# A deformable convolution beside a selective scan: 34 instead of 28 parts of the scan, another PSUM bank for the scan's preparation, weights moved to SBUF, a state matmul issued earlier

## The chip, the core and the metric

The kernel runs on one core of a Trainium2 chip. The metric is the device time of one execution in microseconds; the time before is the median of three runs. All tensors are float32.

## The reference, cut to what matters

Four images of 128 channels and 128 x 128 pixels go through four residual layers, each `x = x + layer(group_norm(x))`:

```python
# layer 0: deformable 3x3 convolution
out = conv3x3(x, offset_w) + offset_b            # 27 values per pixel
dy, dx = clip(out[offsets], -32, 32);  mask = sigmoid(out[mask])
sampled[c, k, h, w] = mask * bilinear(x[c], y = h - 1 + k // 3 + dy, x = w - 1 + k % 3 + dx)
y = einsum('bckhw,ock->bohw', sampled, weight)
# layer 1: 5x7 dilated convolution to 16 channels, then two channel maps
# layer 2: layer norm, depthwise convolutions, a selective scan in four directions:
for t in pixels_in_the_order_of_the_direction:
    h = h * exp(delta[t] * A) + (delta[t] * u[t]) * B[t]     # 128 channels x 16 states
    y[t] = (h * C[t]).sum(over 16 states)
#          layer norm, gate, output projection, layer norm
# layer 3: 3x3 convolution with an edge correction
```

## The kernel before

**The scan is the backbone.** `scan` walks over 4 images x 4 directions x 32 blocks = 512 blocks of 512 pixels. The 128 x 16 states of a block lie in four tiles `h` (128 partitions x 4 x 512, index j), and each tile is scanned in four pieces (index g), one DVE scan instruction each (L1079). So a block has 16 scans, called slots here. For each j the scan needs:

- the input product `h = du * B`: `states_up` (L929) makes the matrix B's rows in the PSUM tile `dub` by two matmuls, and `inputs` (L936) multiplies it into `h`. Three of four run on DVE; the fourth runs on GpSimd (POOL) with a B loaded into SBUF (`bb`), or on DVE as well, see below.
- the decay `exp(delta * A)`: one ACT instruction per slot into a PSUM tile `pa` (L966). Two `pa` banks rotate; a third bank (bank 3) joins them when the work beside the scan leaves it free.
- after its four scans: `carry_on` (L997), the product with C in `outputs` (L1003, `h * cb`, both tiles in SBUF), and `sums` (L977, matmuls into `yacc`).

`prepare(t + 2)` computes delta and delta * u of a later block in small steps, one at each `next(more)`, with three PSUM uses in turn (L873, L889, L901), a copy by ACT (L905) and a product on POOL (L908).

**Beside the scan run the other layers.** They are Python generators, and `together` pulls them in proportion: `around(b)` lists, for each image's 128 blocks, the stages beside them with a weight ("parts"). Beside image 0's scan stand the rest of its own layer2_pre (18 parts), image 1's table (12), and layer 0, layer 1 and layer2_pre of image 1 (28, 14, 36); beside images 1 and 2 stand `tail` of the image before (layer2_post 16, layer 3 with the next table 34) and `head` of the next. A stage gets blocks in the ratio of its parts to the sum. The program order of every engine is then fixed by the order in which the instructions were recorded; nothing is rescheduled at run time, engines wait for each other by semaphores.

`loads("POOL", layer0(st))` sets `beside["busy"] = "POOL"` while layer 0 runs, and the scan then takes DVE instead of POOL for the fourth input product, for `carry_on` and for `outputs` (`c["by"] = nc.vector`). `loads(..., True)` sets `beside["spare"]`, which says that bank 3 may be used by the scan.

**Layer 0** goes over 288 taps (32 blocks of four rows x 9 kernel positions, index n), in a weave of steps:

- `gather`: two tiles `g` of 128 x 2 x 4 x 128, each filled by two indirect DMAs that POOL issues (L447), and for the tap two before, one corner's weighting on POOL (L455);
- `weigh_upper` on ACT (L468), `weigh_lower` on DVE: two instructions per tap, `g[lower] * wl` (L479), where `wl` holds the lower corners' weights of a strip of 16 rows. `lower_weights` (L428) writes `wl` into PSUM bank 2;
- `turn` on TensorE: 16 transposing matmuls (L490) into bank 1 or 3, `copy` by ACT into `smp` (L502), `project` (L510) into bank 0, `add` on DVE (L517, L518) after nine taps.

Ten `g` tiles rotate (20 in the prologue), so POOL can run ahead of the others by some taps. `positions(j + 1)` computes the next strip's sampling points in small steps on TensorE (L359, bank 3), ACT and DVE.

**PSUM.** Eight banks: `dub`, two `pa`, `yacc`, and banks 0 to 3 for the work beside. While layer 0 runs (`beside["full"]`) it holds all four, and `prepare` shares `dub` with `states_up`:

```python
own = beside["own"] = bool(beside.get("spare")) and not beside.get("full")
def place(name):
    return bank(3, name) if own else pss.tile([P, N], F32, name=name, tag="dub")
```

So with `own` false the state matmul for j + 1 is issued at g == 3, one slot ahead, and `sums` at g == 1; with `own` true they are issued at g == 2 and g == 3.

**The prologue** computes layer 0 of image 0 without a scan beside it (L447 to L518 as above), then its layer 1 and the start of layer2_pre; the first scan instruction starts at 2298.6 us.

Of the kernel before, what the change touches and what calls it, by code (L numbers as in the profile page):

```python
# [10 lines left out]
F32 = mybir.dt.float32  # L11
# [7 lines left out]
P = 128  # L19
# [4 lines left out]
N = R * W  # L24
NBLK = H // R
KK = 9
# [5 lines left out]
NG = 4  # L32
# [8 lines left out]
ROWS = 16  # L41
# [71 lines left out]
def conv_preact_kernel(ctx: ExitStack, tc: tile.TileContext, a: dict, nb: int):  # L113
    nc = tc.nc
# [13 lines left out]
    def bank(which, name):  # L128
        return psb.tile([P, N], F32, name=name, tag=f"bank{which}")
# [182 lines left out]
    def layer0(st, pairs=10):  # L312
# [5 lines left out]
        with ExitStack() as s:  # L318
# [18 lines left out]
            def positions(j):  # L337
# [4 lines left out]
                y0 = j * ROWS  # L342
                xs, base, top = got["s", j]

                got["third"] = True
                po = bank(3, "po")
                po3 = po.rearrange("p (r w) -> p r w", w=W)
# [76 lines left out]
            def lower_weights(j):  # L424

                wts = got.pop(("l", j))
                wl = bank(2, "wl")[:, 0 : 2 * ROWS * KK]
                nc.vector.tensor_mul(  # L428
                    wl.rearrange("p (q n) -> p q n", q=2),
                    wts[:, 1:2, 0].to_broadcast([P, 2, ROWS * KK]), wts[:, :, 1],  # L430
                )
                got["p"] = wl.rearrange("p (q r b k) -> p r b k q", q=2, r=R, b=BPS)
# [105 lines left out]
                yield None  # L538
            flush()
            beside["full"] = True  # L540
            while beside.get("own") or beside.get("third"):
                yield None
            fetch_strip(0)
            for n, _ in enumerate(positions(0)):
# [6 lines left out]
                yield share + (1.0 - share) * f  # L551
            flush()
            beside["full"] = False
        st["x1"], st["stats1"] = keep, stats_out


# [260 lines left out]
    def scan(pull):  # L817
# [35 lines left out]
        def prepare(t, early=False):  # L853

            st, k, i, back = seq[t]
            c = blocks[t]
            if (st["b"], k) not in carries:
                carries[st["b"], k] = carry = small.tile([P, NST], F32, name="carry")
                nc.vector.memset(carry, 0.0)
            c["carry"] = carries[st["b"], k]  # L860
            c["bc"] = st["bc"][k % 2][i, k // 2]
            u = c["u"]
            own = beside.get("own")
            beside["prepares"] = own

            def place(name):
                return bank(3, name) if own else pss.tile([P, N], F32, name=name, tag="dub")

            yield None
            if own:  # L870
                yield None
            pdt = place("pdt")
            nc.tensor.matmul(pdt, wd[:, k, :], u, start=True, stop=True)  # L873
            yield None

            dtb = col(V_DTB + k)
            e = sp.tile([P, N], F32, name="e", bufs=1)
            nc.scalar.activation(e, pdt, AF.Abs, bias=dtb)
            above = sp.tile([P, N], F32, name="above", bufs=1)
            nc.scalar.activation(above, pdt, AF.Relu, bias=dtb)  # L880
            yield None
            nc.scalar.activation(e, e, AF.Exp, scale=-1.0)
            yield None
            one_e = sp.tile([P, N], F32, name="one_e", bufs=1)
            nc.scalar.activation(one_e, e, AF.Identity, bias=1.0)
            yield None
            if not back:
                px = place("pxbc")
                nc.tensor.matmul(px, xbc[:, k, :], u, start=True, stop=True)  # L889
            ln = sp.tile([P, N], F32, name="ln", bufs=1)  # L890
            nc.scalar.activation(ln, one_e, AF.Ln)
            yield None
            if not back:
                bc = sp.tile([4 * NST, N], F32, name="bc", bufs=1)
                nc.scalar.copy(bc, px[0 : 4 * NST])  # L895
                store(st["bc"][k][i].rearrange("d j s t -> (d j s) t"), bc)
            nc.scalar.activation(one_e, one_e, AF.Identity, bias=minus)  # L897
            yield from slots(1 if own else 2 if early else 4)
            pd = place("psum")
            for n, (t, sign) in enumerate(((e, ident), (one_e, less), (ln, ident), (above, ident))):  # L900
                nc.tensor.matmul(pd, sign, t, start=n == 0, stop=n == 3)  # L901
            yield from slots(1 if early else 2)
            steps = sp.tile([P, 2, N], F32, name="steps", bufs=1)
            delta, du = steps[:, 0, :], steps[:, 1, :]
            nc.scalar.copy(delta, pd)  # L905
            beside["prepares"] = False
            yield from slots(2 if early else 1)
            nc.gpsimd.tensor_mul(du, delta, u)  # L908
            c["steps"] = sd = dram.tile([P, 2 * N], F32, name="stepsd", bufs=4)
            store(sd, steps.rearrange("p j t -> p (j t)"), 2)  # L910
# [41 lines left out]
        def decay(n):  # L952

            t, n = divmod(n, NST)
            j, g = divmod(n, NG)
            k = seq[t][1]
            turn = (ahead["turn"] + 1) % 3
            if turn == 2 and (not beside.get("own") or beside.get("prepares")):
                turn = 0
            ahead["turn"] = turn  # L960
            if turn == 2:
                beside["third"] = beside.get("third", 0) + 1
                blocks[t]["third", n] = True
            pa = bank(3, "pa3") if turn == 2 else pss.tile([P, N], F32, name="pa", bufs=2)
            at = g * NG + j
            nc.scalar.activation(pa, blocks[t]["d", g], AF.Exp, scale=neg_a[:, k, at : at + 1])  # L966
            blocks[t]["a", n] = pa
# [54 lines left out]
        for t, (st, k, i, back) in enumerate(seq):  # L1022
            c = blocks[t]
            carry = c["carry"]
            on_vector = beside.get("busy") == "POOL"
            own = beside["own"] = bool(beside.get("spare")) and not beside.get("full")
            c["by"] = nc.vector if on_vector else nc.gpsimd
            more = prepare(t + 2, on_vector) if t + 2 < len(seq) else iter(())
            if t > 0:
# [1 line left out]
            for j in range(NG):  # L1031
# [16 lines left out]
                for g in range(NG):  # L1048
                    n = j * NG + g
                    if g == 1:  # L1050
                        decays(at + 1)
                        if t + 1 < len(seq) and j == 3:
                            spread_steps(t + 1, 2)
                            spread_steps(t + 1, 3)
                        if t + 1 < len(seq) and j == (2 if c["by"] is nc.gpsimd else 3):
                            spread_products(t + 1)
                        next(more, None)
                        if before[0] >= 0:
                            carry_on(*before, c["by"])
                            outputs(*before, c["by"])  # L1060
                        if earlier[0] >= 0 and not own:
                            sums(*earlier)
                        if own and j == 2 and t > 0:
                            finish(t - 1)
                    if n and g in (0, 3):
                        next(more, None)
                    if g == 3 and not own and then[0] < len(seq) and not (then[1] == NG - 1 and c["by"] is nc.gpsimd):
                        states_up(*then)
                    if g == 2:
                        decays(at + 2)  # L1070
                        if j == 0 and c["by"] is nc.gpsimd:
                            inputs(t, NG - 1, nc.gpsimd)
                        next(more, None)
                        if own and then[0] < len(seq) and not (then[1] == NG - 1 and c["by"] is nc.gpsimd):
                            states_up(*then)
                    o, f = h[:, g, :], c["a", n]
                    if back:
                        o, f = o[:, ::-1], f[:, ::-1]
                    nc.vector.tensor_tensor_scan(o, f, o, carry[:, n : n + 1], ALU.mult, ALU.add)  # L1079
                    if ("third", n) in c:  # L1080
                        beside["third"] -= 1
                    if g == 3:
                        decays(at + 3)
                        if own and earlier[0] >= 0:
                            sums(*earlier)
                        if not own and j == 1 and t > 0:
                            finish(t - 1)
                    yield (t * NST + n + 1) / total
# [295 lines left out]
    def loads(engine, stage, spare=False):  # L1384
        for f in stage:
            beside["busy"], beside["spare"] = engine, spare
            yield f
        beside["busy"], beside["spare"] = None, False

    def head(b):  # L1390
        st = sts[b]
        table = [(loads(None, layer0_table(st), True), 12)] if b < 2 else []
        return table + [(loads("POOL", layer0(st)), 28), (loads("PE", layer1(st), True), 14),
                (loads("PE", layer2_pre(st), True), 36)]

    def tail(b):
# [117 lines left out]
```

## Time and profile before

| | us |
|---|---|
| median of three runs (20785.77 to 20800.34) | 20786.91 |
| the profiled execution | 20838.75 |
| its span, first to last instruction | 20837.0 |
| mean granted TensorE clock | 0.892 |

| stretch of the span, us | what runs beside the scan | blocks |
|---|---|---|
| 0 to 2298.6 | prologue, no scan | - |
| 2298.6 to 3413.1 | rest of layer2_pre (image 0), table (image 1) | 36 |
| 3413.1 to 5348.7 | layer 0 of image 1 | 33 |
| 5348.7 to 7074.1 | layer 1 and layer2_pre of image 1 | 59 |
| 7074.1 to 8596.4 | layer2_post and layer 3 of image 0, table of image 2 | 51 |
| 8596.4 to 10514.1 | layer 0 of image 2 | 28 |
| 10514.1 to 11986.0 | layer 1 and layer2_pre of image 2 | 49 |
| 11986.0 to 13508.2 | layer2_post and layer 3 of image 1, table of image 3 | 51 |
| 13508.2 to 15424.6 | layer 0 of image 3 | 28 |
| 15424.6 to 16894.4 | layer 1 and layer2_pre of image 3 | 49 |
| 16894.4 to 20837.0 | the last image's scan, layer2_post, layer 3 | 128 |

How to read what follows: PE is TensorE, PEld its weight loads, DVE is VectorE, ACT ScalarE, POOL GpSimd. L447 is line 447 of the kernel before. A row of a stage shows its busy time on each engine with the number of instructions, then the granted clock, the DMA engines' share and GB/s. A group's row shows busy time, the mean of one instruction in ns, and the idle time before the group with what ended it. A timeline row shows start, duration, the instruction and, in brackets, the idle time before it.

### The profile page before, as it was taken

Reading aid. Unit: us, or ns where it says so; the run is one execution under the profiler, and the core shown is the slowest. Engines: PE = TensorE matmul, PEld = TensorE weight load, DVE = VectorE, ACT = ScalarE, POOL = GpSimd, SP = SyncE. Lnnn points to the kernel's source line nnn. Section 1 sums busy time; section 2 is a strip of 40 time slices with the busy share of each in tenths; the row PEclk is TensorE's granted clock in tenths of the full one; section 3 lists DMA queues with packets and bytes.
Section 4 is the critical chain, followed back from the end, with each engine's and each line's share of the span. In section 5 each row is a group of like instructions: output and inputs, shape, how many; then the busy total and the mean of one; then the engine's idle time right before and its main releaser. Section 6 shows DMA issues by size and latency. Waiting matters only on the chain.

```text
span 20837.0 us, 209864 instructions
## 1 busy us (share of the span) xinstructions
PE 15847.0 (76%) x58778; PEld 6719.5 (32%) x58778; DVE 16855.7 (81%) x14665; ACT 12887.2 (62%) x25086; POOL 16827.5 (81%) x10597
## 2 busy tenths in 40 slices
PE   4667776777878888777778887877777877677778
PEld 2444222444322223344422222244432222122223
DVE  1222588888999899888899889978889998999983
ACT  3444566666667666566667776666666767655563
POOL 4775577888788888888878888888878889999994
PEclk7888888998989999899999998988998988899899
DMA  7666678777767877777777796777776777555673
GB/s 234 192 193 191 193 229 283 259 255 253 245 205 225 235 236 254 239 247 251 247 235 224 225 250 229 253 244 248 248 241 221 235 216 221 185 185 195 197 219 120
DMA packets 2909354, 4717.50 MB, mean 226 GB/s; under 512 B 1095248, under 2 KB 1369240, under 8 KB 2831264
## 3 DMA queue, kind: packets, MB, share of 16 engines
q1 hardware_dynamic: 2539552, 3495.83, 52.5%
q0 software_dynamic: 368640, 1208.25, 18.8%
q8 instruction: 476, 7.80, 0.1%
q14 instruction: 686, 5.62, 0.1%
HBM read 3766.27 MB, written 908.60 MB: 224 GB/s over the span
## 4 chain that ended last, share of the span: by engine, by line
DVE 34%; PE 19%; issue 12%; DMA 11%; ACT 10%; POOL 8%; another core or an unknown queue 3%; SPq 2%; DVEq 0%; POOLq 0%; ACTq 0%
DVE h L1079 20%; DVE h L936 11%; PE pst L490 4%; PE psum L901 4%; POOL g L447 3%; DMA du<-stepsd 3%; ACT pa L966 3%; DMA g<-table,idx 2%; PE acc L510 2%; ACT g L468 2%; DMA delta<-stepsd 2%; PE p L1309 1%; POOL h L1003 1%; PE yacc L977 1%
## 5 line engine op out<-in xcount | busy, mean ns | idle before, releaser
L1079 DVE TENSOR_TENSOR_SCAN h<-pa,carry,h 128x512 f32<-128x512 f32 x8192 | 10005.1, 1267 | 767.6 <-ACT pa L966 571.5
L966 ACT ACTIVATE pa<-delta,neg_a 128x512 f32<-128x512 f32 x8192 | 5538.0, 687 | 4751.5 <-DVE h L1079 3700.4
L1003 POOL TENSOR_TENSOR h<-h,cb 128x2048 f32<-128x2048 f32 x1692 | 7670.5, 4533 | 137.0 <-POOL carry L997 0.6
L447 POOL DMA_INDIRECT g<-table,idx x4608 | 4874.2, 1058 | 1679.5 <-issue 1136.4
L936 DVE TENSOR_TENSOR h<-du,dub 128x2048 f32<-128x2048 f32 x1625 | 3684.3, 2267 | 826.4 <-PE dub L929 310.3
L490 PE MATMUL pst<-ident,g 128*128 128x128 f32 x18432 | 2670.0, 299 | 1665.1 <-issue 644.8
L929 PE MATMUL dub<-u,xb_sb 128*128 128x512 f32 x3250 | 2047.3, 716 | 1713.3 <-DVE h L936 1529.8
L490 PEld LDWEIGHTS pst<-ident,g 128*128 128x128 f32 x18432 | 2312.0, 155 | 2699.8 <-issue 1297.6
L468 ACT ACTIVATE g<-g,wt 128x128 f32<-128x128 f32 x8072 | 2577.6, 392 | 216.7 <-DMA g<-table,idx 162.4
L977 PE MATMUL yacc<-h,gather_sb 128*32 128x512 f32 x16384 | 2364.6, 650 | 87.0 <-POOL h L1003 61.0
L936 POOL TENSOR_TENSOR h<-du,bb 128x2048 f32<-128x2048 f32 x423 | 1927.4, 4557 | 18.1 <-DMA du<-stepsd 18.1
L479 DVE TENSOR_TENSOR g<-g,wl 128x512 f32<-128x512 f32 x2304 | 1488.2, 669 | 359.9 <-DMA g<-table,idx 315.4
L502 ACT COPY smp<-pst 128x512 f32<-128x512 f32 x1152 | 664.8, 577 | 1569.9 <-remote 1013.2
L929 PEld LDWEIGHTS dub<-u,xb_sb 128*128 128x128 f32 x3250 | 598.4, 210 | 2877.1 <-DVE h L936 2211.9
L510 PE MATMUL acc<-smp,w_sb 128*128 128x512 f32 x2304 | 1371.3, 679 | 133.2 <-DVE x L517 60.9
L908 POOL TENSOR_TENSOR steps<-steps,u 128x512 f32<-128x512 f32 x512 | 652.5, 1274 | 909.5 <-ACT steps L905 905.2
L1309 PE MATMUL p<-xn,w_l_sb 128*128 128x508 f32 (+2 forms) x2304 | 1149.6, 620 | 1.8 <-ACT xn L1288 1.8
L977 PEld LDWEIGHTS yacc<-h,gather_sb 128*32 128x32 f32 x16384 | 338.3, 112 | 1838.1 <-issue 1315.9
L901 PE MATMUL psum<-e,ident 128*128 128x512 f32 x1024 | 613.8, 684 | 357.6 <-ACT bc L895 338.0
L901 PE MATMUL psum<-one_e,less 128*128 128x512 f32 x1024 | 639.1, 711 | 310.7 <-ACT one_e L897 310.1
L517 DVE TENSOR_TENSOR x<-acc,xres 128x512 f32<-128x512 f32 x128 | 87.1, 680 | 966.5 <-remote 525.3
L455 POOL TENSOR_SCALAR g<-g,wt 128x128 f32<-128x128 f32 x1144 | 833.0, 728 | 37.4
(170 smaller groups left out, 18122.0 us busy)
## 6 DMA issues: line engine op xcount, KB each, us to landing
cb<-bcd SPq DMA_DIRECT2D x512, 1024.0 KB
delta<-stepsd SPq DMA_DIRECT2D x2048, 256.0 KB
du<-stepsd SPq DMA_DIRECT2D x2048, 256.0 KB
stepsd<-steps SPq DMA_DIRECT2D x512, 512.0 KB
table<-gt SPq DMA_DIRECT2D x512, 256.0 KB
bb<-bcd SPq DMA_DIRECT2D x512, 256.0 KB
win<-nd SPq DMA_DIRECT2D x512, 160.0 KB
g<-table,idx POOLq DMA_INDIRECT x4608
```

What stands on the lines that cost most here:

```text
L447: nc.gpsimd.indirect_dma_start(out=g[:, r].rearrange("p q c -> p (q c)"), out_offset=None, in_=table, in_offset=bass.IndirectOffsetOnAxis( ...
L468: nc.scalar.activation(g, g, AF.Copy, scale=w)
L479: nc.vector.tensor_mul(g, g, wl.unsqueeze(3).to_broadcast([P, 2, 2, P]))
L490: nc.tensor.matmul(pst[:, r * P : (r + 1) * P], g[:, r % 2, q, :], ident, start=q == 0, stop=q == 3, is_transpose=True,)
L510: nc.tensor.matmul(got["a", i], w0[:, k, :], got.pop(("c", n)), start=k == 0, stop=k == KK - 1)
L901: nc.tensor.matmul(pd, sign, t, start=n == 0, stop=n == 3)
L929: nc.tensor.matmul(p, xb[:, seq[t][1], j, :], c["u"], start=True, stop=True)
L936: engine.tensor_mul(h, c["du"], b.unsqueeze(1).to_broadcast([P, NG, N]))
L966: nc.scalar.activation(pa, blocks[t]["d", g], AF.Exp, scale=neg_a[:, k, at : at + 1])
L977: nc.tensor.matmul(c["y"][g * Q : (g + 1) * Q, :], gather, c["h", j][:, g, :], start=j == 0, stop=last and not second,)
L1003: engine.tensor_mul(h, h, c["cb"][:, j, :].unsqueeze(1).to_broadcast([P, NG, N]))
L1079: nc.vector.tensor_tensor_scan(o, f, o, carry[:, n : n + 1], ALU.mult, ALU.add)
```

## The change

Layer 0 gets 34 parts of the scan instead of 28, the other stages keep theirs. `wl` becomes an SBUF tile. Bank 2, which this frees while layer 0 runs, takes the three PSUM uses of `prepare`; `own` is now the number of the bank (2 beside layer 0, 3 where bank 3 is spare, 0 otherwise). With `own == 2` the state matmul for j + 1 is issued at g == 1, three slots before its use. `sums` and `finish` follow the branch that `own` selects, so beside layer 0 they are issued at g == 3 and at j == 2. `positions` first copies out whatever transposed tap is still in PSUM, and layer 0 ends only when a running `prepare` has left bank 2.

```diff
@@ positions
+                for n in [key[1] for key in got if key[0] == "t" and isinstance(key, tuple)]:
+                    copy(True)(n)
                 got["third"] = True
                 po = bank(3, "po")
@@ lower_weights
-                wl = bank(2, "wl")[:, 0 : 2 * ROWS * KK]
+                wl = mp.tile([P, 2 * ROWS * KK], F32, name="wl")
@@ layer0
-            while beside.get("own") or beside.get("third"):
+            while beside.get("own") == 3 or beside.get("third"):
                 yield None
...
             beside["full"] = False
+            while beside.get("own") == 2 and beside.get("prepares"):
+                yield None
@@ prepare
-                return bank(3, name) if own else pss.tile([P, N], F32, name=name, tag="dub")
+                return bank(own, name) if own else pss.tile([P, N], F32, name=name, tag="dub")
@@ decay
-            if turn == 2 and (not beside.get("own") or beside.get("prepares")):
+            if turn == 2 and (beside.get("own") != 3 or beside.get("prepares")):
@@ scan
-            own = beside["own"] = bool(beside.get("spare")) and not beside.get("full")
+            own = beside["own"] = 2 if beside.get("full") else 3 if beside.get("spare") else 0
+            beside["prepares"] = own if t + 2 < len(seq) else 0
...
                         next(more, None)
+                        if own == 2 and then[0] < len(seq):
+                            states_up(*then)
                         if before[0] >= 0:
                             carry_on(*before, c["by"])
                             outputs(*before, c["by"])
...
-                        if own and then[0] < len(seq) and not (then[1] == NG - 1 and c["by"] is nc.gpsimd):
+                        if own == 3 and then[0] < len(seq) and not (then[1] == NG - 1 and c["by"] is nc.gpsimd):
                             states_up(*then)
@@ head
-        return table + [(loads("POOL", layer0(st)), 28), (loads("PE", layer1(st), True), 14),
+        return table + [(loads("POOL", layer0(st)), 34), (loads("PE", layer1(st), True), 14),
```

## The prediction

> **What bounds the kernel now.** I read the totals, then busy time by stage, then the groups and waits inside the deformable layer, then a stretch of the timeline.
>
> ```profile
> PE 15847.0 (76%) x58778; PEld 6719.5 (32%) x58778; DVE 16855.7 (81%) x14665; ACT 12887.2 (62%) x25086; POOL 16827.5 (81%) x10597
> ```
> DVE and POOL tie as an average, so they must be parted by stage. Busy time by stage (columns: length, then PE, PEld, DVE, ACT, POOL):
>
> ```profile
> 3413.10:5348.70 1935.60, 1474.73 (x7505) 821.72 (x7505) 1701.94 (x1709) 1253.74 (x3141) 1547.07 (x1475) 0.90 0.76 249
> 5348.70:7074.10 1725.40, 1381.45 (x4113) 455.97 (x4113) 1616.84 (x1225) 1164.74 (x1839) 1490.19 (x623) 0.91 0.70 226
> 8596.40:10514.10 1917.70, 1414.08 (x7249) 794.58 (x7249) 1519.37 (x1573) 1181.15 (x3008) 1496.61 (x1470) 0.89 0.74 241
> 10514.10:11986.00 1471.90, 1217.50 (x3609) 410.21 (x3609) 1366.75 (x1030) 1013.38 (x1597) 1248.91 (x524) 0.92 0.73 232
> ```
> Rows 1 and 3 are layer 0 of images 1 and 2 beside the scan; rows 2 and 4 are layer 1 and layer2_pre behind it. Counting scans (16 to a block), they hold 33, 59, 28 and 49 blocks. Layer 0 takes the same time over 33 blocks (1935.6 us) as over 28 (1917.7): it doesn't go by blocks. The other stretch does: 1725.4 - 1471.9 = 253.5 us for ten blocks, 25.35 us each. There DVE's scans set the pace (94% busy).
>
> What holds layer 0? Its inner part, 3490 to 5300 us (1810 us), POOL's groups (busy, mean ns, idle before them):
>
> ```profile
> L447 POOL DMA_INDIRECT g<-table,idx x1118 | 1242.4, 1111 | 304.1 <-issue 244.9 <-DMA g<-table,idx 8.7 <-DVE h L1079 8.0
> L455 POOL TENSOR_SCALAR g<-g,wt 128x128 f32<-128x128 f32 x279 | 216.1, 775 | 9.1
> L908 POOL TENSOR_TENSOR steps<-steps,u 128x512 f32<-128x512 f32 x31 | 39.6, 1279 | 0.0
> ```
> Busy plus idle is 1811 us, all of it, and the idle is some 0.27 us before each gather: POOL never waits for anybody. **POOL is the bound of layer 0.** DVE in the same window:
>
> ```profile
> DVE h L936 <- PE dub L929: 69.8, 35, 8.9
> DVE h L936 <- issue: 57.8, 31, 8.0
> ```
> These waits (152 us with the smaller ones) are what the earlier state matmul is to remove, but on the engine that isn't the bound.
>
> The timeline shows what slows POOL:
>
> ```profile
> 4401.52 0.95 POOL L447 DMA_INDIRECT g<-table,idx  x1 [0.30 <-issue]
> 4403.29 3.06 POOL L447 DMA_INDIRECT g<-table,idx  x1 [0.17 <-issue]
> 4406.66 0.95 POOL L447 DMA_INDIRECT g<-table,idx  x1 [0.30 <-issue]
> ...
> 4403.18 2.29 DVE L1003 TENSOR_TENSOR h<-h,cb 128x2048 f32<-128x2048 f32 x1
> 4406.59 0.66 DVE L479 TENSOR_TENSOR g<-g,wl 128x512 f32<-128x512 f32 x1
> ```
> A gather that starts under DVE's L1003, whose two inputs (h, cb) both lie in SBUF, takes 3.06 instead of 0.95 us; one beside L479, whose wl lies in PSUM, keeps 0.95. That contrast decides this case, because the change moves wl to SBUF. In the prologue, without L1003, a gather takes 964 ns and an L455 626. So L1003 costs POOL here (1242.4 - 1118 x 0.964) + (216.1 - 279 x 0.626) = 206 us for 124 of them, 1.66 us each.
>
> **The change, part by part.** The sum starts from the profiled execution: 20838.75 us, of which 20837.0 is span; the median of the runs is 20786.91, 51.8 lower. I apply the difference to the median.
>
> *34 parts for layer 0.* In the built order the blocks with L1003 on DVE go from 33, 28, 28 to 38, 33, 33; five blocks per image leave the other stages. There each is worth 25.35 us by the two rows above; layer2_pre alone gives 25.5 (42 blocks in 1225.7 us, 35 in 1047.0). A block beside layer2_post (34 us, DVE busy 32) hangs less on the scans, so I take 24: 15 x 24 = -360 (-315 to -380). In layer 0 a block more costs POOL four L1003 and one L908: 4 x 1.66 + 1.28 = 8 us, so 40 per image; the trace's own pair gives 18 for five blocks (1935.6 against 1917.7), as a short layer 0 starts with a crowded block of 124 us. I take 40 + 25 + 25 = +90 (54 to 120).
>
> *Lower weights in SBUF.* L428 writes SBUF instead of PSUM: nothing. The 576 L479 per image now have two SBUF inputs. Duration: L936 (one input in PSUM) has a mean of 2283 ns, L1003 (both SBUF) at best 2291, so L479 stays at 0.66 to 0.69. The price is POOL's. In the trace a gather that starts at least 0.05 us into an L1003 ends as if it had started 0.12 us before the L1003's end. Laid over the recorded L479s, that rule catches some 260 of 576 per image, 0.27 us each: 70 us. Counting L479s that stand back to back as one gives 87 to 101. The short two-input operations of the position computation (0.45 us) lose POOL about 40 ns each, which by the square of the window beyond the first 0.17 us is 0.13 us for 0.69, or 75. I take 80: 3 x 80 = +240. Ends: 40 ns each, the short row unscaled (3 x 23), and 3 x 110.
>
> The Trainium skill (SBUF — State Buffer, "Who interferes with whom") says that a DVE instruction with two SBUF inputs contends with a GpSimd instruction that reads SBUF but not with one that only writes, and infers that descriptor generation needs only the write side. By that page only L455, one POOL operation in five, would be hit, an estimate of 15 us per image, and the total would be about 200 us faster. The 3.06 us gather speaks against the inference here, and the row decides.
>
> *Prologue.* Image 0's layer 0 has no scan beside it: no gain, but 576 L479. POOL there has waits of some 3 us per nine taps (2.13 and 1.37 us in one stretch), so the same 70 us is partly covered: +35 (0 to 70). DVE's L479s come there in bursts, 17 in 10.23 us after a wait for L517. Whether POOL gets in between two of a burst no row shows; that is rival C.
>
> *Preparation in bank 2, state matmul at g == 1, sums at g == 3.* These lift at most DVE's 152 us (image 1) or 224 us (image 2) of L936 waits, which POOL hides: 0. Without that cover the gain would be those waits. The matmul L929 waits for L936 of the same j, which stands before scan 0, so it is free at g == 1; behind it queue the transposes L490, and they wait for POOL anyway. The later sums hold one of five h tiles two scans longer: 0; exposed, at most the 3 us per L936 that the longer waits show.
>
> *Copies before positions* move eight ACT copies of 0.57 us per image: 0, as ACT is 66% busy; behind an early copy queue the decays, which now wait on DVE. *The wait at the end of layer 0* holds layer 1 back about 0.4 block; such a block takes 42 us instead of 26 (block 206 of before), so some 6 us per image, which the faster pull afterwards gives back: 0 (to 20).
>
> *Is DVE late next?* Image 1: 38 blocks x 39.7 us (16 x 1.275, 4 x 2.28, 4 x 2.33, carries 0.9) = 1509, L479 397, the rest of the layer 95: 2001, less 5% of overlap (the groups sum to 1690 in a window of 1605 busy) = 1900. POOL: 288 taps x 5.59 (4 x 1.234 + 0.65) = 1610, blocks 38 x 8 = 304, L479 80, ends 50: 2044. POOL stays the bound, DVE at 93%; +15 for the coupling (0 to 60).
>
> Sum: -360 + 90 + 240 + 35 + 15 = **+20 us**, 20859 profiled, **20807 as median**. About 0.2% (42 us) is what a measurement of this kernel can tell from no change.
>
> **The rivals.** *B, the lock hardly bites* (23 us an image, 10 in the prologue): -360 + 90 + 69 + 10 + 15 = -176, 20611. For it: the short two-input rows lose only 40 ns, and wl is broadcast in its last dimension, which no two-input row shows. Against: 3.06 us under L1003.
>
> *C, bursts shut POOL out* (slower): a DVE burst of two-input operations holds the shared port from one L479 to the next. Then every burst of 17 costs POOL its 10 us less 3 of slack, 32 bursts: +225 instead of +35, and 95 instead of 80 beside the scan: +45. Total 20 + 190 + 45 = +255, 21042; with the stall also slowing the chain behind, to +330. It decides as soon as a POOL operation waits longer than one L479. For it: the burst of 17; against: a gather needs the port only for a moment.
>
> *D, DVE becomes the bound of image 1*: if its 11% of waits stay, 1900 / 0.89 = 2135 against 2044, so +75 net: 20880. For it: 93% load; against: the waits shrank from 300 to 205 us where the load grew.
>
> **How the numbers follow.** A holds 0.50, its own range 20700 to 20910 (the bounds of the lock and of the price of a block); of it 0.15 falls below -0.2%, 0.17 within, 0.18 above. B 0.20 (0.19 faster, 0.01 same), C 0.25 and D 0.05 (slower). Faster 0.34, same 0.18, slower 0.48. The range reaches to B's centre and C's long end: 20600 to 21120.
>
> **What would show it.** Layer 0 of image 1 at some 2040 us over 38 blocks, of images 2 and 3 at 2020 over 33; POOL again without waits there; gathers under an L479 at 1.2 to 1.5 us where they began inside it; layer 1 plus layer2_pre at 24 to 25 us per block less. The prologue tells A from C: 2330 or 2520 instead of 2298.6 us to the first scan. A gather mean unchanged at 0.96 in the prologue would be B. I am wrong altogether if POOL waits in layer 0 or DVE's L936 waits prove to set its time.

## The result, and the profile after

The changed kernel takes 20819.23 us (median of 20 runs, 20804.16 to 20836.59), the kernel before 20786.58 in 20 runs beside it: a ratio of 1.0015, interval 1.0008 to 1.0022. The forecast was 20807 with a range of 20600 to 21120. Its profiled execution took 20823.53 us, span 20821.8, which is 4 above its median; the one of before lay 52 above its own.

The totals moved little:

```profile
PE 15832.9 (76%) x58808; PEld 6696.5 (32%) x58808; DVE 17147.3 (82%) x14800; ACT 12901.1 (62%) x25086; POOL 16903.7 (81%) x10462
```

By stage they moved a great deal. Busy time of the changed kernel by stage, the rows that answer to those of before (length, then PE, PEld, DVE, ACT, POOL): layer 0 of image 1, layer 1 and layer2_pre of image 1, and the same two of image 2.

```profile
3356.40:5427.30 2070.90, 1555.82 (x7765) 825.62 (x7765) 1914.74 (x1849) 1330.20 (x3262) 1679.47 (x1478) 0.90 0.76 245
5427.30:7051.00 1623.70, 1332.47 (x3963) 439.72 (x3963) 1535.45 (x1167) 1119.55 (x1769) 1418.36 (x595) 0.92 0.73 231
8502.90:10536.80 2033.90, 1491.18 (x7507) 815.43 (x7507) 1732.41 (x1710) 1261.67 (x3129) 1627.77 (x1475) 0.89 0.75 239
10536.80:11965.50 1428.70, 1192.79 (x3511) 407.06 (x3511) 1311.88 (x995) 984.38 (x1552) 1198.06 (x504) 0.92 0.75 233
```

All stages, from the first scan of each block:

| stage | before, us (blocks) | after, us (blocks) | difference |
|---|---|---|---|
| prologue | 2298.6 | 2273.6 | -25.0 |
| rest of layer2_pre, table | 1114.5 (36) | 1082.8 (34) | -31.7 |
| layer 0, image 1 | 1935.6 (33) | 2070.9 (38) | +135.3 |
| layer 1, layer2_pre | 1725.4 (59) | 1623.7 (56) | -101.7 |
| layer2_post, layer 3 | 1522.3 (51) | 1451.9 (48) | -70.4 |
| layer 0, image 2 | 1917.7 (28) | 2033.9 (33) | +116.2 |
| layer 1, layer2_pre | 1471.9 (49) | 1428.7 (47) | -43.2 |
| layer2_post, layer 3 | 1522.2 (51) | 1451.8 (48) | -70.4 |
| layer 0, image 3 | 1916.3 (28) | 2031.7 (33) | +115.4 |
| layer 1, layer2_pre | 1469.9 (49) | 1428.5 (47) | -41.4 |
| last scan and what follows | 3942.6 (128) | 3944.3 (128) | +1.7 |

The stages that the 15 blocks left gave 358.8 us, the three layers 0 took 366.9. So the change is two large effects that cancel.

POOL's groups in the inner part of layer 0 of image 1 (3420 to 5380 us, 1960 us; busy, mean ns, idle before them):

```profile
L449 POOL DMA_INDIRECT g<-table,idx x1130 | 1350.5, 1195 | 306.3 <-issue 220.9 <-DMA g<-table,idx 17.2 <-DVE h L1086 11.2
L457 POOL TENSOR_SCALAR g<-g,wt 128x128 f32<-128x128 f32 x283 | 249.4, 881 | 9.3
L912 POOL TENSOR_TENSOR steps<-steps,u 128x512 f32<-128x512 f32 x36 | 45.9, 1275 | 0.0
```
Busy and idle again make up the whole window, with 0.27 us of idle per gather, so POOL is still the bound; a gather now means 1195 ns instead of 1111, the corner product 881 instead of 775. DVE's waits in the same window:

```profile
DVE g L481 <- DMA g<-table,idx: 61.5, 42, 4.2
DVE h L940 <- PE dub L933: 22.8, 15, 3.0
```
The waits of the state product for `dub` fell from 70 to 23 us, and those of L481 for gathers rose from 23 to 62: DVE waits for POOL.

What a gather meets under a lower-weight product, in the timeline of the changed kernel (start, duration):

```profile
4038.37 1.03 POOL L449 DMA_INDIRECT g<-table,idx  x1 [0.31 <-issue]
4039.70 1.47 POOL L449 DMA_INDIRECT g<-table,idx  x1 [0.30 <-issue]
4041.47 1.47 POOL L449 DMA_INDIRECT g<-table,idx  x1 [0.31 <-issue]
...
4039.69 0.66 DVE L481 TENSOR_TENSOR g<-g,wl 128x512 f32<-128x512 f32 x1
4040.27 1.27 DVE L1086 TENSOR_TENSOR_SCAN h<-pa,carry,h 128x512 f32<-128x512 f32 x1
4041.46 0.66 DVE L481 TENSOR_TENSOR g<-g,wl 128x512 f32<-128x512 f32 x1
```
A gather that starts 0.01 us after an L481 takes 1.47 instead of 0.95 us. Here a product and a scan on DVE take 1.77 us, a delayed gather with its 0.30 us of issue also 1.77, so the next gather starts at the next L481 again.

That gathers crowd at the start of a product is not new, though. Of an image's 1152 gathers, 66, 53 and 65 begin within 0.05 us of an L479's start in the profile of before, and they lose nothing there, as here with 0.02 us between the two starts:

```profile
4475.63 0.95 POOL L447 DMA_INDIRECT g<-table,idx  x1 [0.30 <-issue]
...
4475.61 0.66 DVE L479 TENSOR_TENSOR g<-g,wl 128x512 f32<-128x512 f32 x1
```
In the changed kernel 102, 81 and 87 begin so, and each loses 0.51 us.

### The profile page after: what moved, and what is told of

The parts are those of the page before. It is cut to its first block, busy times and chain, and to the rows that moved or that the text cites. A ratio compares the mean times of both kernels' runs of the same rounds, so it can differ in the third digit from the quotient of the medians.

```text
span 20821.8 us, 209810 instructions
## 1 busy us (share of the span) xinstructions
PE 15832.9 (76%) x58808; PEld 6696.5 (32%) x58808; DVE 17147.3 (82%) x14800; ACT 12901.1 (62%) x25086; POOL 16903.7 (81%) x10462
## 4 chain that ended last, share of the span: by engine, by line
DVE 32%; PE 18%; DMA 14%; issue 12%; POOL 10%; ACT 9%; SPq 2%; another core or an unknown queue 2%; DVEq 0%; POOLq 0%; ACTq 0%
DVE h L1086 18%; DVE h L940 10%; POOL g L449 6%; DMA g<-table,idx 6%; PE psum L905 4%; ACT pa L970 3%; DMA du<-stepsd 3%; PE pst L492 2%; DMA delta<-stepsd 2%; PE acc L512 2%; PE p L1316 1%; ACT g L470 1%; POOL g L457 1%; DVE g L481 1%
## 5 line engine op out<-in xcount | busy, mean ns | idle before, releaser
L1007 POOL TENSOR_TENSOR h<-h,cb 128x2048 f32<-128x2048 f32 x1632 | 7398.9, 4534 | 131.8 <-POOL carry L1001 0.8
L449 POOL DMA_INDIRECT g<-table,idx x4608 | 5231.0, 1135 | 1602.8 <-issue 987.0
L492 PEld LDWEIGHTS pst<-ident,g 128*128 128x128 f32 x18432 | 2260.9, 153 | 3065.4 <-POOL g L457 1535.0
L481 DVE TENSOR_TENSOR g<-g,wl 128x512 f32<-128x512 f32 x2304 | 1634.8, 721 | 1106.4 <-DMA g<-table,idx 881.3
L940 POOL TENSOR_TENSOR h<-du,bb 128x2048 f32<-128x2048 f32 x408 | 1859.4, 4557 | 19.6 <-DMA du<-stepsd 16.3
L512 PE MATMUL acc<-smp,w_sb 128*128 128x512 f32 x2304 | 1417.4, 702 | 70.7 <-DVE x L519 42.0
L1007 DVE TENSOR_TENSOR h<-h,cb 128x2048 f32<-128x2048 f32 x416 | 954.9, 2296 | 14.3
L457 POOL TENSOR_SCALAR g<-g,wt 128x128 f32<-128x128 f32 x1144 | 905.3, 791 | 37.6
```

The lines of the kernel that those rows point to most:

```text
L449: nc.gpsimd.indirect_dma_start(out=g[:, r].rearrange("p q c -> p (q c)"), out_offset=None, in_=table, in_offset=bass.IndirectOffsetOnAxis( ...
L481: nc.vector.tensor_mul(g, g, wl.unsqueeze(3).to_broadcast([P, 2, 2, P]))
L492: nc.tensor.matmul(pst[:, r * P : (r + 1) * P], g[:, r % 2, q, :], ident, start=q == 0, stop=q == 3, is_transpose=True,)
L512: nc.tensor.matmul(got["a", i], w0[:, k, :], got.pop(("c", n)), start=k == 0, stop=k == KK - 1)
L940: engine.tensor_mul(h, c["du"], b.unsqueeze(1).to_broadcast([P, NG, N]))
L1007: engine.tensor_mul(h, h, c["cb"][:, j, :].unsqueeze(1).to_broadcast([P, NG, N]))
```

## The experiments

Each run was timed against the kernel before on the same chip. The chips differ: the kernel before has medians of 20691.79, 20821.12, 20698.84 and 20830.01 us on the four that were used, and the prologue, where its work is the same, takes 2184 to 2299 us to the first scan. So stages are compared, and totals only as ratios. "The lock" is, as in the prediction, the time that POOL is held up while DVE runs an instruction with two inputs in SBUF.

**1. The kernel before again.**

> The kernel before once more, for a second profile. The changed kernel's profile reaches the first scan at 2273.6 us, the first profile of before at 2298.6, though the changed kernel's gathers lose 61 us more there under L479. Theory 1, an edit of the change speeds the prologue up: the first scan again at about 2298 us. Theory 2, the prologue varies from one execution to the next: another time, down to about 2250 us (the first profile lay 52 us above the median of the runs). The stages after it should repeat within 5 us each under both.

The prologue took 2184.6 us instead of 2298.6; all stages after it but layer 0 repeat within 4 us, layer 0 (1929.8, 1907.5, 1908.8) only within 6 to 10, where I had expected 5. Theory 2: the prologue varies. What goes with it is seen beside the run of experiment 8, which has the same prologue work but for the early copies. First each run's busy time between 300 and 1800 us, with the granted clock third from the end, then TensorE's costliest group; experiment 1:

```profile
300.00:1800.00 1500.00, 953.22 (x5280) 638.79 (x5279) 452.92 (x716) 748.62 (x2155) 1200.39 (x1340) 0.90 0.70 203
```
```profile
L490 PE MATMUL pst<-ident,g 128*128 128x128 f32 x4288 | 640.8, 298 | 544.6 <-POOL g L455 538.3 <-ACT smp L502 6.2
```
and experiment 8:

```profile
300.00:1800.00 1500.00, 947.75 (x5052) 681.91 (x5048) 393.38 (x687) 668.40 (x2042) 1131.53 (x1264) 0.81 0.67 192
```
```profile
L492 PE MATMUL pst<-ident,g 128*128 128x128 f32 x4064 | 638.2, 324 | 438.6 <-ACT smp L504 259.0 <-issue 179.4
```
At a granted clock of 0.90 the transposes wait for POOL, which bounds the prologue; at 0.81 they wait for ACT's copies, in the loop of transposes, copy and projection, and POOL has slack. The clock was 0.81 in the first profile of before as well. That the clock is the cause is my reading of these profiles; no run sets it.

**2. 34 parts alone.**

```diff
-        return table + [(loads("POOL", layer0(st)), 28), (loads("PE", layer1(st), True), 14),
+        return table + [(loads("POOL", layer0(st)), 34), (loads("PE", layer1(st), True), 14),
```


> The kernel before with 34 instead of 28 parts for layer 0 and nothing else. Theory A (POOL bounds layer 0, five blocks per image leave the scan-bound stages): -360 there, +40 +25 +25 in layer 0 and +15 for the coupling, so about -255 us, some 20530; layer 0 of image 1 takes about 1975 us over 38 blocks, of images 2 and 3 about 1940 over 33. Theory D (DVE becomes the bound of image 1, since here the state matmul still comes one slot ahead): layer 0 of image 1 at 2080 to 2135 us, the total near -130, some 20655.

20524.07 us, 0.9917 (0.9903 to 0.9930): a gain of 168, between theory A's 255 and theory D's 130 and nearer to D. Against experiment 1 the other stages gave 369 us and layer 0 took +112.9, +40.2 and +40.2. For images 2 and 3 that is the 40 of four L1003 and one L908 per block. Image 1 took 2042.7 us, between the theories. Its waits there (3420 to 5350 us, 1930 us), POOL's and DVE's:

```profile
POOL steps L908 <- ACT steps L905: 109.6, 27, 27.5
```
```profile
DVE h L936 <- PE dub L929: 111.5, 73, 7.4
```
Here POOL does wait: for the scan's preparation, up to 27.5 us at a time, while DVE is busy 1792.48 of 1930 us and has `dub` in use late. I read this as DVE setting the time of image 1 at 38 blocks, with the preparation sharing `dub`, and dragging POOL along; no run parts DVE's load from its waits for `dub`.

**3. The lower weights in SBUF alone.**

```diff
-                wl = bank(2, "wl")[:, 0 : 2 * ROWS * KK]
+                wl = mp.tile([P, 2 * ROWS * KK], F32, name="wl")
```


> The kernel before with the lower weights in an SBUF tile and nothing else. Theory A (the second SBUF input of L479 holds POOL up): as in the changed kernel's profile, where operations of POOL that begin under an L479 lose 126, 110 and 111 us in the three images, so +330 to +350 beside the scan, in layer 0 alone, and between -27 and +60 in the prologue: 21090 to 21200. As it stood in the prediction: +275, 21062. Theory B (the lock hardly bites, the loss of the changed kernel lies in the bank or the order): within 30 us of before.

21012.99 us, 1.0158 (1.0144 to 1.0171): 321 us lost. Layer 0 took 100.0, 87.7 and 81.8 us more than in experiment 1, the prologue 47.1 more, and the sum of all other stages moved 18 us the other way. POOL's operations that begin under an L479 lose 115.6, 97.5 and 94.6 us there, those under L1003 some 20, 5 and 11 less than in experiment 1. Theory B is out. This one line and the blocks add up to the loss of the change: with the 40 us that five blocks cost images 2 and 3 of experiment 2, it makes 140, 128 and 122 us, where experiment 5 has 141.8, 124.8 and 133.4. In layer 0 it cost less than the 330 to 350 us that I expected from the first profile (269.5 in all); with the prologue it is 317, where the prediction's terms say 275.

**4. The early copies alone.**

```diff
+                for n in [key[1] for key in got if key[0] == "t" and isinstance(key, tuple)]:
+                    copy(True)(n)
```


> The kernel before with the early copy of a transposed tap before the positions and nothing else. Theory 1 (this copy frees TensorE in the prologue, where it waits 296 us for ACT's copies): the first scan some 25 us earlier, the total near -27, 20760; beside the scan nothing, as POOL is the bound. Theory 2 (the copies are worth nothing): within 10 us of before.

1.0002 (0.9993 to 1.0011), first scan at 2186.2 against 2184.6: nothing. Theory 2.

**5. The changed kernel again.**

> The changed kernel once more, for a profile from the same chip as those it is compared with here. Theory A: against the second profile of before, layer 0 of the three images longer by 140, 126 and 125 us, the prologue by 40 to 50 (as with the weights in SBUF alone, 2231.7 against 2184.6), the other stages shorter by some 360 in all, as in the first profile: +30 to +80. If the prologue of the changed kernel is really shorter by an edit, it stays 25 under that of before.

1.0010 (1.0001 to 1.0019). Layer 0 took 2071.6, 2032.3 and 2042.2 us: 141.8, 124.8 and 133.4 more than in experiment 1. The prologue, 2294.7, can't be set against that run's, whose clock was higher; experiment 8 on this chip has 2295.9 with the weights in PSUM, so here the SBUF weights cost the prologue nothing.

**6. The whole change at 28 parts.**

```diff
-        return table + [(loads("POOL", layer0(st)), 34), (loads("PE", layer1(st), True), 14),
+        return table + [(loads("POOL", layer0(st)), 28), (loads("PE", layer1(st), True), 14),
```


> The whole change, but with 28 parts. It differs from the run with the weights in SBUF alone (1.0158 of before) by the bank, the earlier state matmul and the order of the sums. Theory A (POOL covers DVE's waits, so these are worth nothing here): within 40 us of that run, 1.014 to 1.018. Theory E (the bank and the earlier matmul are worth some 70 to 100 us in every image, as the difference between 34 parts alone, the weights alone and the whole change suggests when simply added): 1.002 to 1.006.

1.0120 (1.0105 to 1.0136), below the band named for A and above E's. Layer 0 took 2029.2, 1987.6 and 1980.7 us, against 2029.8, 1995.2 and 1990.6 in experiment 3. So bank, earlier matmul and later sums are worth 0 to 10 us per image at 28 parts, as A says; most of the rest of the difference is the prologue (2295.0 us, against 2295.9 in experiment 8 with the weights in PSUM), where the lock cost nothing on this chip.

**7. The lower-weight product in two halves** (the whole change otherwise).

```diff
-                    nc.vector.tensor_mul(g, g, wl.unsqueeze(3).to_broadcast([P, 2, 2, P]))
+                    for r in range(2):
+                        nc.vector.tensor_mul(g[:, r], g[:, r], wl[:, r].unsqueeze(2).to_broadcast([P, 2, P]))
```


> The changed kernel with each product by the lower weights issued as two instructions of half the length (0.42 us instead of 0.69, 128 x 256 each). If the port is given up between two such instructions, POOL loses less per image, by the square of the window some 40 to 60 us instead of 110 in images 2 and 3: layer 0 there some 55 us shorter. If a run of two-input instructions keeps it, the pair is a window of 0.85 us and POOL loses 150 to 190: layer 0 there 40 to 80 us longer. Image 1 has 80 us more of DVE work and should be longer either way.

0.9950 (0.9937 to 0.9964): the changed kernel with more instructions beats the changed kernel by 0.6%. POOL's loss under the products fell to some 70 us per image (71, 67 and 66), layer 0 to 2034.1, 2000.1 and 1998.5. Mostly POOL gets in between two products that stand back to back: of 416 gathers beside the scan that began under a half which another half followed at once, 391 went on when the first one ended, 25 later. It isn't always so. In the prologue a run of 19 halves held one gather for 5.30 us:

```profile
442.72 6.45 DVE L482 TENSOR_TENSOR g<-g,wl 128x256 f32<-128x256 f32 x19
...
444.75 5.30 POOL L449 DMA_INDIRECT g<-table,idx  x1 [1.99 <-issue]
```
A second one took 3.80 us there, and two of 8.77 and 6.21 us stand in the prologue of experiment 12. The size is less than I expected (32 and 44 us instead of 55 in images 2 and 3), and image 1, which I held to be longer either way, is 37.5 shorter: POOL, not DVE, still set it.

**8. 34 and 42 parts, weights in PSUM** (with the copies of experiment 4).

```diff
-        return table + [(loads("POOL", layer0(st)), 28), (loads("PE", layer1(st), True), 14),
+        return table + [(loads("POOL", layer0(st)), 34 if b < 2 else 42), (loads("PE", layer1(st), True), 14),
```


> The kernel before with 34 parts for layer 0 of image 1 and 42 for images 2 and 3, weights left in PSUM, with the early copies (worth nothing by themselves). Theory A with what 34 parts alone showed: image 1 as there (layer 0 2043 us over 38 blocks); images 2 and 3 now also get 38 blocks and come to DVE's limit, some 2040 us of layer 0 (+93 against 34 parts) for five blocks less elsewhere (-117): 25 us each gained over 34 parts alone, so 0.989 of before. Rival: the stages that are left get too dense to give 23 us a block, and it is 0.992 or worse.

0.9864 (0.9849 to 0.9879), better than 34 parts alone. Layer 0 of images 2 and 3 took 2008.6 and 2006.7 us over 37 blocks (I had expected 2040 over 38), some 60 more than over 33, and the other stages kept giving (1365.2 and 1370.7 us for 45 blocks).

**9. The corner of L455 on ACT** (the kernel before otherwise).

```diff
-                    if h == 1 and n >= 2:
-                        g, w = neighbour(n - 2, h, 1, 1)
-                        nc.gpsimd.tensor_scalar(g, g, w, None, ALU.mult)
...
-                            if h == 1 and r == 1 and c == 1 and n + 2 < NBLK * KK:
-                                continue
```


> The kernel before (28 parts, weights in PSUM) with the one corner that POOL weights (L455) weighted by ACT like the other three of the upper row. Theory A (POOL is the bound of layer 0): 288 times 0.65 us and what L1003 adds to them leave POOL, so layer 0 of images 2 and 3 some 195 us shorter (1720), until DVE is the bound; image 1, where DVE is 88% busy, 110 to 150 shorter; total 0.973 to 0.978 with the prologue between 0 and -100. Rival (something else holds layer 0 at 1910 us whatever POOL does, the gathers' transfers or TensorE): within 60 us of before.

20088.58 us, 0.9709 (0.9696 to 0.9723): the best version found, faster than both kernels. Layer 0 took 1825.8, 1739.0 and 1734.2 us (-104, -169, -175 against experiment 1), the prologue 2016.8 (-168). That is more than I expected in the total (0.973 to 0.978), because of the prologue, and less in layer 0 (110 to 150 in image 1, 195 in images 2 and 3). POOL still bounds image 2, though some of its idle time now ends with ACT and with gathers' transfers (8280 to 9840 us, 1560 us), where its two groups' busy and idle make 1561:

```profile
L447 POOL DMA_INDIRECT g<-table,idx x1093 | 1194.8, 1093 | 331.3 <-issue 177.3 <-ACT g L463 29.1 <-DMA g<-table,idx 28.7
L903 POOL TENSOR_TENSOR steps<-steps,u 128x512 f32<-128x512 f32 x26 | 33.4, 1285 | 2.0 <-ACT steps L900 1.6
```

**10. The same with 30 and 36 parts.**

```diff
-        return table + [(loads("POOL", layer0(st)), 28), (loads("PE", layer1(st), True), 14),
+        return table + [(loads("POOL", layer0(st)), 30 if b < 2 else 36), (loads("PE", layer1(st), True), 14),
```

> As the run before it, with 30 parts for layer 0 of image 1 and 36 for images 2 and 3. Theory A: images 2 and 3 come to DVE's limit at 34 blocks, layer 0 some 100 us longer than with 28 parts for 144 us less elsewhere; image 1 a loss of 30. So 60 us better than the run before it, 0.970 to 0.975. Rival: DVE is already the bound there at 28 parts, every block more costs 40 us in layer 0 and gives 24 elsewhere: 150 us worse than the run before it.

0.9708 (0.9695 to 0.9722), the same as experiment 9: layer 0 took 93, 111 and 109 us more, the other stages gave as much. Both expectations missed; with POOL relieved the number of parts no longer matters around here.

**11. The state matmul one slot ahead again** (the changed kernel otherwise).

```diff
-                        if own == 2 and then[0] < len(seq):
-                            states_up(*then)
...
+                    if g == 3 and own == 2 and then[0] < len(seq):
+                        states_up(*then)
```


> The changed kernel with the state matmul beside layer 0 one slot ahead (g == 3) again, the bank kept. Theory A (POOL covers DVE's waits): layer 0 of images 2 and 3 within 10 us of the changed kernel (2032, 2042); image 1, where DVE is 94% busy, 20 to 60 us longer than 2071, as the waits of L936 come back. Rival (the earlier slot carries the difference between 34 parts alone and the whole change): image 1 longer by 70 us or more and the others by 30 or more.

Layer 0: 2072.1, 2040.5, 2034.7 us, against 2071.6, 2032.3, 2042.2 in experiment 5. DVE's waits in image 1 came back (3380 to 5330 us):

```profile
DVE h L940 <- PE dub L933: 129.5, 66, 5.2
```
and cost nothing, in image 1 neither, where I had expected 20 to 60. The earlier matmul is worth nothing here, where POOL is the bound. (The total, 1.0042 with 1.0028 to 1.0056, comes from a chip with a high clock: its prologue took 2231.5 us, as in experiment 3.)

**12. The whole change with the corner on ACT** (the edit of experiment 9 in the changed kernel).

```diff
-                    if h == 1 and n >= 2:
-                        g, w = neighbour(n - 2, h, 1, 1)
-                        nc.gpsimd.tensor_scalar(g, g, w, None, ALU.mult)
...
-                            if h == 1 and r == 1 and c == 1 and n + 2 < NBLK * KK:
-                                continue
```

> The whole change (34 parts, bank 2, weights in SBUF) with the corner of L455 weighted by ACT, so that POOL has room beside layer 0. Theory A (what the change lost was POOL's time, the bank is worth DVE's waits once DVE is the bound): POOL still loses 90 to 110 us per image under the products by the lower weights, but behind DVE; layer 0 of images 2 and 3 at 1800 to 1830 us over 33 blocks, 20 to 50 less than with 30 and 36 parts and the weights in PSUM (1849.7, 1843.2); the prologue 0 to 50 longer than there; total 0.967 to 0.973, against 1.001 of the change without this edit. Rival (the lock's loss stays whole, as POOL is still nearly full): layer 0 of images 2 and 3 at 1920 or more, the total 0.977 or worse.

0.9858 (0.9841 to 0.9874). The prologue took 2308.5 us, so I compare layer 0: 1924.6 and 1932.1 us over 33 blocks, 75 to 89 more than in experiment 10 with the weights in PSUM. The rival holds. POOL loses 184, 150 and 150 us under the products here, more than with its corner products: 241, 176 and 189 gathers per image now begin within 0.05 us of a product's start.

The prologue is worth a look, too. It took 14 us more than in experiment 5 (2294.7), although POOL has no corner products any more, while the same edit gave 168 us in experiment 9. The clock is low again:

```profile
300.00:1800.00 1500.00, 907.76 (x5010) 644.49 (x5008) 391.65 (x680) 730.69 (x2268) 988.75 (x999) 0.80 0.66 190
```
In experiment 9 it was 0.92 there. I read from it that 168 us of that experiment's gain hang on a prologue that POOL bounds. (The weights lie in SBUF here and in PSUM there; experiments 5 and 8 saw no price of that at the low clock.)

## Why the prediction was right, point by point

**The blocks that leave the other stages: right.** -360 was said, -358.8 measured, -369 in experiment 2. That both kernels hold these stages with DVE's scans could be read from two rows.

**POOL as the bound of layer 0: right.** Its busy and idle fill the window before and after, and experiments 9, 3 and 11 show it from three sides: time taken off POOL comes back, time put on it is paid, and DVE's waits cost nothing. The exception is image 1 of experiment 2, where POOL waited for the scan's preparation.

**The lock: right in kind, too small.** +240 was said; POOL lost 126, 110 and 111 us under L481, together 347, above the upper end that I had given (3 x 110). The term that was mis-sized is the rule laid over the recorded products of before: it found 260 hits of 0.27 us per image, the changed kernel has 308, 284 and 273 of 0.41, 0.39 and 0.41.

The rule had its edge from L1003, where a gather must begin at least 0.05 us into the product to be held: the 12 that began earlier beside the scan of before lost 0.01 us each. Under L481 there is no such edge. Its 270 gathers of the first 0.05 us lost 138 us, 40% of all, and the rule left their like out. With the edge for gathers at 0 it gives 98, 92 and 99 us on the profile of before, 289 in all (64, 64 and 65 with the old edge); on experiment 1 it gives 111, 87 and 90, where experiment 3 measured 115.6, 97.5 and 94.6. On experiment 2, with 34 parts, it gives 303. Up to 347 some 44 us are left; that the lock itself shifts more gathers to the start of a product (270 instead of experiment 2's 224) fits them, but wasn't tried by itself. DVE paid as well: an L481 has a mean of 728 ns in the inner part of image 1, an L479 664, where 0.66 to 0.69 us was said; off the bound that cost nothing.

**The blocks in layer 0: too dear.** +90 was said. Losses under L1003 (L1007 after) went from 210 to 213, 166 to 182 and 167 to 178 us, +31; 15 more L908 cost 19. That is 50. The 40 us too many and the 107 too few partly cancel, and the +15 for the coupling of DVE and POOL did not show, so layer 0 came to +367 instead of +345 in the first pair of profiles and to +400 in the second (experiment 5 against 1). The crowded first block of images 2 and 3, by which the prediction explained its own low pair, did get shorter (124 and 131 us before, 70 and 73 after), but that gave layer 0 next to nothing: between its first and its last gather it grew by 374 us, outside them it shrank by 7.

**Bank, earlier matmul, later sums at nothing: right here, for the reason given.** Experiments 6 and 11 show it, both with POOL slowed by the lock. What DVE's waits can cost without that cover shows in experiment 2: at 38 blocks with `dub` shared, image 1 loses some 70 us more than its blocks cost POOL. Whether the bank would give that back is not shown. In the changed kernel POOL's own price (the lock's 100 us and the blocks' 40) already makes up image 1's 141.8, so it needs no saving by the bank. Nor were the bank, the order of the sums and the preparation's steps, which `own` shifts as well, tried one by one.

**The skill's inference.** The Trainium skill (SBUF — State Buffer, "Who interferes with whom") infers that descriptor generation needs only the write interface and is spared by a two-input product. Experiment 3 settles it for these gathers: one line that makes the second input SBUF costs 82 to 100 us per image, and gathers of 0.95 us take 1.47. What of the gather is held, its reading of the indices from SBUF or the writing of descriptors, no run shows.

**The prologue: right in size on one chip, nothing on another.** +35 was said, with 0 to 70; it is +47 where the clock is 0.88 to 0.90 (experiments 3 and 1) and 0 where it is 0.80 to 0.81 (experiments 5 and 8). In the first pair of profiles it is even -25, at 0.82 against 0.81; that stays open. Rival C falls in size: POOL lost some 40 to 60 us in the prologues with the weights in SBUF, not 225. Its mechanism is not unreal, though. Single operations in the prologues of experiments 5 and 6 waited 0.9 and 1.0 us, more than one product, which was to decide for C and did not; and experiments 7 and 12 have the four gathers of 3.8 to 8.8 us that runs of products, with short two-input operations between them, shut out.

**The sum.** +20 was said, +32.6 measured by the medians. That it came so close is partly luck: the lock was 107 us dearer, the blocks 40 and the coupling 15 cheaper, and the prologue's 35 were not there. The two profiles alone say -15: -358.8 + 366.9 - 25.0 + 1.7, as the first one lay 52 us above its median. Which stage of it was slow can't be told from one profile; the prologue is the one stage that varies so much.

## What to carry to other kernels

Before an operand moves from PSUM to SBUF, ask whether the instruction then has two SBUF inputs on DVE, and whether GpSimd is the bound beside it: here that line alone cost 1.6%, while the regrouping it was made for was worth nothing. Price each engine's waits by the engine that bounds that stage; take work from that one first (one product per tap moved to ACT gave 2.9%, 0.8 of it in the prologue, which gained nothing on a chip with the lower clock). And when a change is a bundle, its parts want to be run alone: 34 parts without the rest gave 0.8%.

## What the runs showed of the hardware that I had not expected

- How early a gather must begin to escape the lock differs by the product: under the 0.66 us product with two SBUF inputs 270 gathers that began in its first 0.05 us lost 0.51 us each, under the 2.29 us one 12 such gathers lost 0.01 us each.
- The same two-input product in two halves of 0.44 us costs POOL some 70 us per image instead of 110 to 126, and the kernel 0.6% less. Between two such halves 391 of 416 gathers got in, but a run of 19 held one for 5.30 us.
- The granted TensorE clock of the prologue (0.81 or 0.90 between 300 and 1800 us) goes with the engine that bounds it: the same edit cost 0 or 47 us there, and another gave 0 or 168.
